# Token rows drifting a tile behind the counts, layers in blocks of two tiles, and table splitting spread over two tiles, in a recommendation kernel

## The chip, the cores and the metric

The kernel runs on one core of one Trainium2 chip. The metric is device time in microseconds (us) of one execution, as the median of several runs, lower being better. Two other numbers go with it: the span of one profiled execution (first to last instruction), and the mean granted clock of the matrix engine, where 1.0 is full speed. Engine names are those of the profile: PE (matrix), PEld (its weight loads), DVE (vector), ACT (scalar), POOL (GpSimd, which issues the gathers here), SP (issues plain DMAs). L318 means line 318 of that kernel; the changed kernel has other line numbers than the kernel before.

## The reference, cut to what matters

For each of 16,384 rows the model averages 32 word vectors of 300 columns from a table of 50,000 rows, averages 20 rows each of three tables of 64 columns, takes one row each of four small tables, and feeds 748 columns through three layers to one sigmoid. A "wide" sum of one-column tables is added to the last logit.

```python
tok = word_emb[token_idx].mean(axis=1)          # 32 of 50000 x 300
e1, e2, e3 = (emb_mh_i[mh_i_idx].mean(axis=1))  # 20 each of 1000, 5000, 10000 x 64
o1 ... o4 = emb_oh_i[oh_i_idx]                  # 100, 50, 20, 1000 x 64
emb = concatenate([tok, e1, e2, e3, o1, o2, o3, o4], axis=1)
wide = sum over all small tables of their wide column, at the same indices
h = relu(emb @ W1 + b1)   # 748 -> 1024
h = relu(h @ W2 + b2)     # -> 512
h = relu(h @ W3 + b3)     # -> 256
return sigmoid(h @ Wd + bd + wide)
```

## The kernel before

A tile is 128 batch rows, and there are 128 of them. The small tables stay in SBUF, split into three bf16 terms. Lookups in them are done as counting (one-hot matrices from DVE, products on PE into `pc`, evicted by ACT as `cnt`) followed by sums of table slices weighted with the counts (PE into `pg`). Word vectors are too many for that: they are gathered by 32 indirect DMAs per tile and added on DVE. Everything is put out in 11 steps per tile, so that each engine has something of each kind to do all the time. In step-tile t, counts belong to tile t, sums to tile t-1 and layers to a block of tiles finished before.

The token part starts a tile's gathers with its counts and adds each group of two rows three groups later:

```python
tokp = tile_pool(name="tok", bufs=2 * TOK_LAG)        # 6 buffers of two rows
def tokens(t, it):
    for q in range(n_groups):                          # 16 groups of 2 gathers
        rows = tokp.tile([P, TOK_GROUP * TOK_D], F32)
        for r in range(TOK_GROUP):
            nc.gpsimd.indirect_dma_start(out=rows[:, r * TOK_D : ...], in_=word, ...)
        under_way.append((t, q, rows))
        if len(under_way) > TOK_LAG:
            add_up(*under_way.pop(0))                  # two DVE additions
        yield 1
# ... in each step i of tile t:
toks.to(n_groups * (i + 1) / STEPS)
```

The layers take blocks of four tiles (512 columns) and, at the end, of two, one and one:

```python
def transposed(x, gs):
    for k in range(NK):                                # 6 chunks of features
        pt = ps_h.tile([P, BLOCK], F32, tag="ph")      # PSUM, 2 buffers
        for s, g in enumerate(gs):
            nc.tensor.transpose(pt[:kk, s * P : (s + 1) * P], chunk(g, k), ident)
        nc.vector.tensor_scalar(x[:kk, k, 0:n], pt[:kk, 0:n], scale[:kk, k : k + 1], None, ALU.mult)
        yield CHUNK_WORK
def layer(dst, weights, bias, src, kks, n_out, n):
    for m in range(n_out):
        ph = ps_h.tile([P, BLOCK], F32, tag="ph")
        for k, kk in enumerate(kks):
            nc.tensor.matmul(ph[:, 0:n], weights[...], src[:kk, k, 0:n], ...)
        nc.scalar.activation(dst[:, m, 0:n], ph[:, 0:n], AF.Relu, bias=...)
sizes = [NSUB] * (tiles // NSUB - 1) + [NSUB - 2, 1, 1]
```

The splitting of the small tables (18 ACT and 12 DVE operations) is done inside tile 0, and counts are evicted with `AF.Copy, scale=0.5, saturate=True`.

## Time and profile before

| | kernel before |
|---|---|
| time, median of 3 runs | 5295.36 us (5286.8 to 5298.4) |
| span of the profiled run, clock | 5284.0 us, 0.991 |
| busy: PE, POOL, DVE, ACT | 96%, 73%, 71%, 48% |
| step-tile 3 begins | 152.5 us |
| step-tile 3 to 125, per tile | 40.06 us |
| from step-tile 125 to the end | 243.9 us |

The last three rows are read from PE's timeline: a new step-tile begins where the 128 count matmuls of the one before are done.

PE is the busiest engine, so one would call it the bound. The chain of work that ended last, followed back from the last instruction, says otherwise (first lines of that view, shares of the span):

```profile
PE 26%; DMA 26%; issue 17%; DVE 17%; POOL 12%; ACT 1%; SPq 0%; DVEq 0%; POOLq 0%; ACTq 0%
```

Only a quarter of the chain is PE. Most of the rest is the loop of gather, landing and addition. The group of DVE's token additions (columns: engine and operation, shapes, count, then busy time and mean duration, then idle time before them and what ended most of it) shows DVE waiting for landings:

```profile
L214 DVE TENSOR_TENSOR own<-own,tok_rows 128x300 f32<-128x300 f32 x1792 | 857.1, 478 | 715.5 <-DMA tok_rows<-in_word_emb_dram,it 684.8
```

Of its idle time 684.8 us end with a landing. Keep this line in mind: it is the one that changes most.

### The profile page before, as it was taken

Reading aid. Unit: us, or ns where it says so; the run is one execution under the profiler, and the core shown is the slowest. Engines: PE = TensorE matmul, PEld = TensorE weight load, DVE = VectorE, ACT = ScalarE, POOL = GpSimd, SP = SyncE. Lnnn points to the kernel's source line nnn. Section 1 sums busy time; section 2 is a strip of 40 time slices with the busy share of each in tenths; the row PEclk is TensorE's granted clock in tenths of the full one; section 3 lists DMA queues with packets and bytes.
Section 4 is the critical chain, followed back from the end, with each engine's and each line's share of the span. In section 5 each row is a group of like instructions: output and inputs, shape, how many; then the busy total and the mean of one; then the engine's idle time right before and its main releaser. Section 6 shows DMA issues by size and latency. Waiting matters only on the chain.

```text
span 5284.0 us, 104301 instructions
## 1 busy us (share of the span) xinstructions
PE 5073.1 (96%) x41320; PEld 3160.4 (60%) x41320; DVE 3763.4 (71%) x8014; ACT 2528.4 (48%) x2000; POOL 3881.2 (73%) x4103
## 2 busy tenths in 40 slices
PE   3699999999999999999999999999999999999999
PEld 3556565666565666666566556556656556655658
DVE  6777777777777777777777777777777777777753
ACT  5444444444444444444444445445444444444433
POOL 5777777777777777777777777777777777777762
PEclk9799999999999999999999999999999999999999
DMA  6444444444444444444444444444444444444431
GB/s 167 125 124 126 126 126 126 126 125 125 126 126 126 126 124 126 126 125 126 125 125 125 126 126 125 124 125 126 125 126 125 124 126 125 126 126 125 124 103 34
DMA packets 245354, 652.60 MB, mean 124 GB/s; under 512 B 108977, under 2 KB 111988, under 8 KB 244863
## 3 DMA queue, kind: packets, MB, share of 16 engines
q0 software_dynamic: 196608, 629.41, 43.4%
q1 hardware_dynamic: 48255, 16.53, 1.4%
q8 instruction: 323, 5.29, 0.4%
q14 instruction: 168, 1.38, 0.1%
HBM read 645.59 MB, written 0.07 MB: 122 GB/s over the span
## 4 chain that ended last, share of the span: by engine, by line
PE 26%; DMA 26%; issue 17%; DVE 17%; POOL 12%; ACT 1%; SPq 0%; DVEq 0%; POOLq 0%; ACTq 0%
DMA tok_rows<-in_word_emb_dram,it 25%; PE ph L387 14%; POOL tok_rows L223 12%; PE pg L336 8%; DVE own L214 5%; DVE own L212 3%; PE pc L311 3%; DVE slice L293 3%; DVE row L293 1%; DVE x L378 1%; DVE g L342 1%; DVE own L210 1%; PE po L412 1%; DMA raw<-in_mh_dram 0%; ACT cnt L318 0%
## 5 line engine op out<-in xcount | busy, mean ns | idle before, releaser
L223 POOL DMA_INDIRECT tok_rows<-in_word_emb_dram,it x4096 | 3880.3, 947 | 1324.0 <-issue 754.2
L318 ACT ACTIVATE cnt<-pc 128x1656 fp8e3<-128x1656 f32 (+1 forms) x1408 | 2120.6, 1506 | 2020.2 <-PE pc L311 2004.1
L336 PE MATMUL pg<-terms,cnt 128*128 128x195 bf16 x17664 | 1847.6, 254 | 83.1 <-DVE g L342 81.4
L336 PEld LDWEIGHTS <-cnt 128*128 128x128 fp8e3 x17664 | 1599.5, 144 | 229.1 <-issue 74.9
L387 PE MATMUL ph<-x,w_sb 128*128 128x512 f32 (+5 forms) x3264 | 1458.3, 576 | 0.5 <-DVE x L378 0.5
L214 DVE TENSOR_TENSOR own<-own,tok_rows 128x300 f32<-128x300 f32 x1792 | 857.1, 478 | 715.5 <-DMA tok_rows<-in_word_emb_dram,it 684.8
L387 PE MATMUL ph<-h,w_sb 128*128 128x512 f32 (+2 forms) x2720 | 1211.0, 573 | 0.0
L212 DVE TENSOR_TENSOR own<-own,tok_rows 128x300 f32<-128x300 f32 x1920 | 918.5, 478 | 400.3 <-DMA tok_rows<-in_word_emb_dram,it 348.6
L311 PEld LDWEIGHTS <-row 64*128 64x128 bf16 x16384 | 504.5, 95 | 1083.3 <-DVE own L214 255.7
L293 DVE TENSOR_TENSOR row<-own,sc 128x768 bf16<-128x768 bf16 (+1 forms) x1408 | 761.3, 541 | 156.5 <-PE pc L311 81.7
L311 PE MATMUL pc<-slice,row 64*128 64x138 bf16 x16384 | 759.1, 224 | 115.0 <-ACT cnt L318 72.2
L387 PEld LDWEIGHTS ph<-x,w_sb 128*128 128x128 f32 (+1 forms) x3264 | 560.3, 193 | 397.8 <-issue 394.0
L293 DVE TENSOR_TENSOR slice<-own,sc 128x828 bf16<-128x828 bf16 (+1 forms) x1408 | 796.2, 565 | 0.0
L387 PEld LDWEIGHTS ph<-h,w_sb 128*128 128x128 f32 x2720 | 463.1, 192 | 318.4 <-issue 316.3
L396 ACT ACTIVATE h<-ph,b_sb 128x512 f32<-128x512 f32 (+2 forms) x476 | 315.3, 662 | 684.8 <-PE ph L387 673.1
L342 DVE TENSOR_REDUCE g<-pg 128x130 f32<-128x390 f32 (+1 forms) x512 | 258.1, 504 | 108.7 <-PE pg L336 108.3
L378 DVE TENSOR_SCALAR x<-pt,scale 128x512 f32<-128x512 f32 (+4 forms) x204 | 137.2, 713 | 5.3 <-PE pt L377 3.4
L377 PE MATMUL pt<-ident,g 128*128 128x128 f32 (+1 forms) x768 | 103.2, 275 | 2.8 <-DVE x L378 2.3
L210 DVE TENSOR_TENSOR own<-tok_rows 128x300 f32<-128x300 f32 x128 | 61.5, 480 | 47.5 <-DMA tok_rows<-in_word_emb_dram,it 44.6
L377 PEld LDWEIGHTS pt<-ident,g 128*128 128x128 f32 (+1 forms) x768 | 85.5, 140 | 6.4 <-DVE x L378 5.4
L214 DVE TENSOR_TENSOR g<-own,tok_rows 128x300 f32<-128x300 f32 x128 | 60.2, 470 | 25.9 <-DMA tok_rows<-in_word_emb_dram,it 21.1
L412 PE MATMUL po<-h,wd_sb 128*1 128x512 f32 (+2 forms) x136 | 60.9, 566 | 0.3
(34 smaller groups left out, 369.1 us busy)
## 6 DMA issues: line engine op xcount, KB each, us to landing
tok_rows<-in_word_emb_dram,it POOLq DMA_INDIRECT x4096
ix<-in_idx_dram SPq DMA_DIRECT2D x128, 32.0 KB
w_sb<-in_W_dram SPq DMA_DIRECT2D x6, 512.0 KB
it<-in_idx_dram SPq DMA_DIRECT2D x32, 64.0 KB
w_sb<-in_W_dram SPq DMA_DIRECT2D x1, 2048.0 KB
raw<-in_mh_dram SPq DMA_DIRECT2D x1, 975.0 KB
out_dram<-h SPq DMA_DIRECT2D x31, 2.0 KB
raw<-in_mh_dram SPq DMA_DIRECT2D x1, 292.5 KB
```

Of the source, the lines that this page charges most:

```text
L212: nc.vector.tensor_add(tok_sum, tok_sum, a)
L214: nc.vector.tensor_add(to, tok_sum, b)
L223: nc.gpsimd.indirect_dma_start(out=rows[:, r * TOK_D : (r + 1) * TOK_D], out_offset=None, in_=word, in_offset=bass.IndirectOffsetOnAxis(ap ...
L293: nc.vector.tensor_tensor(one[:, 0:rows, :].rearrange("p i (n d) -> p i n d", d=2), iota[:, 0:n].rearrange("p (n d) -> p n d", d=2).unsque ...
L311: nc.tensor.matmul(pc[:, f, k // n, at : at + n_h], hot[0][half, k, :], hot[1][half, k, :], start=True, stop=True,)
L318: nc.scalar.activation(cnt[:, :, b : b + rows, :].rearrange("l f (g k) h -> l f g (k h)", g=2), pc[:, :, :, 0 : n * n_h], AF.Copy, scale=0 ...
L336: nc.tensor.matmul(pg[:, j, :], by_slice[:, :, h], terms[:, h, :], start=(h == h0), stop=(h == h1 - 1))
L342: nc.vector.tensor_reduce(g[:, at : at + n * ROW].rearrange("p (f d) -> p f d", f=n), pg[:, 0:n, :].rearrange("p f (c d) -> p f d c", c=3) ...
L377: nc.tensor.transpose(pt[:kk, s * P : (s + 1) * P], chunk(g, k), ident)
L378: nc.vector.tensor_scalar(x[:kk, k, 0:n], pt[:kk, 0:n], scale[:kk, k : k + 1], None, ALU.mult)
L387: nc.tensor.matmul(ph[:, 0:n], weights[:kk, k, m * P : (m + 1) * P], src[:kk, k, 0:n], start=(k == 0), stop=(k == len(kks) - 1),)
L396: nc.scalar.activation(dst[:, m, 0:n], ph[:, 0:n], AF.Relu, bias=bias[:, m : m + 1])
```

## The change

Four things change together. (1) Token groups become one stream over the whole run, spread over 129 step-tiles instead of 128, so that tokens drift slowly until they are a tile behind the counts; eight row buffers instead of six. (2) Layers come in blocks of two tiles (256 columns) throughout, so that less is left over at the end and layers begin earlier. (3) The table splitting is spread over two tiles, with 1.2 of ACT's copies (and the subtraction ahead of each, where there is one) per step from the fourth step on; the weights are loaded a tile later. (4) The saturation flag of the count eviction goes.

```diff
+TOK_BUFS = 8
+LAYER_BLOCK = 256
-CHUNK_WORK = 1
-LAYER_TIME = 10
+CHUNK_WORK = 0.5
+TABLE_PACE = 1.2
+LAYER_TIME = 5
...
-    PART, CHUNK = n_h // 3, n_h // 6
+    PART = n_h // 6
...   (splitting: one ACT copy per yield, DVE's subtraction ahead of it)
+                if c:
+                    nc.vector.scalar_tensor_tensor(rows, rows, 2.0 if c == 1 else 1.0, term[c - 1], ...)
+                nc.scalar.activation(term[c], rows, AF.Copy, scale=2.0 if c == 0 else 1.0)
+                yield 1
...
+    n_all = B // P * n_groups + TOK_LAG
-    def tokens(t, it):
+    def tokens():
+        for n in range(n_all):
+            if n < n_all - TOK_LAG:
+                ... two gathers of group n ...
+            if n >= TOK_LAG:
+                add_up(*under_way.pop(0))
...
-            saturate=True,
+            saturate=False,
...
-            pt = ps_h.tile([P, BLOCK], F32, name="pt", tag="ph")
+            pt = ps_h.tile([P, LAYER_BLOCK], F32, name="pt", tag="ph")
...   (the same for ph, x, h1, h2, h3, po)
-    sizes = [NSUB] * (tiles // NSUB - 1) + [NSUB - 2, 1, 1]
...
-                toks.to(n_groups * (i + 1) / STEPS)
+            toks.to(n_all * (t * STEPS + i + 1) / ((tiles + 1) * STEPS))
-                if t == 0 and i % 3:
-                    next(tables_on_chip, None)
-                if t == 0 and i == STEPS - 1:
+                tables_on_chip.to(TABLE_PACE * (t * STEPS + i - 2))
+                if t == 1 and i == STEPS - 1:
                     load_weights()
```

## The prediction

> **What bounds the kernel now.** One core walks 128 tiles of 128 batch rows in 11 steps each. A step counts lookups (PE into `pc`, ACT evicts), sums table slices (PE into `pg`), runs some matmuls of the layers, and adds gathered token rows on DVE; 32 gathers per tile are issued on POOL. I read the page's groups first, then the windows, then POOL's and PE's timelines in mid run and near both ends.
>
> ```profile
> L223 POOL DMA_INDIRECT tok_rows<-in_word_emb_dram,it x4096 | 3880.3, 947 | 1324.0 <-issue 754.2
> L336 PE MATMUL pg<-terms,cnt 128*128 128x195 bf16 x17664 | 1847.6, 254 | 83.1 <-DVE g L342 81.4
> L387 PE MATMUL ph<-x,w_sb 128*128 128x512 f32 (+5 forms) x3264 | 1458.3, 576 | 0.5 <-DVE x L378 0.5
> ```
> ```profile
> 0.00:50.00 50.00, 6.95 (x88) 5.13 (x88) 26.74 (x59) 24.57 (x17) 23.16 (x29) 1.00 0.76 183
> 1000.00:2000.00 1000.00, 985.86 (x8006) 603.62 (x8003) 729.25 (x1553) 489.07 (x384) 756.35 (x800) 1.00 0.46 125
> ```
> ```profile
> 2021.84 0.94 POOL L223 DMA_INDIRECT tok_rows<-in_word_emb_dram,it  x1 [0.30 <-DVE own L214]
> 2023.09 0.95 POOL L223 DMA_INDIRECT tok_rows<-in_word_emb_dram,it  x1 [0.30 <-issue]
> 2024.34 0.95 POOL L223 DMA_INDIRECT tok_rows<-in_word_emb_dram,it  x1 [0.30 <-DVE own L214]
> ```
>
> PE is busy 98.6% of that window, POOL only 75.6%, and yet POOL is the bound. Gathers start every 1.25 us (0.95 busy, 0.30 between), 800 per 1000 us, with no longer gap from about 76 to 5084 us. 32 x 1.25 = 40.0 us per tile, 4096 x 1.25 = 5120 us in all. PE is a hair behind it, as the timeline's start-to-start distances show (records overlap, so their means do not):
>
> ```profile
> 2020.95 0.54 PE L311 MATMUL pc<-slice,row 64*128 64x138 bf16 x12
> 2021.43 1.52 PE L336 MATMUL pg<-terms,cnt 128*128 128x195 bf16 x15
> 2022.78 1.91 PE L387 MATMUL ph<-x,w_sb 108*128 108x512 f32 x4
> 2024.62 0.54 PE L311 MATMUL pc<-slice,row 64*128 64x138 bf16 x12
> ```
>
> 12 counts take 0.475 us, 15 sums 1.36 (0.085 each and 0.09 handover), four layer records of 512 columns 1.84 (0.432 each and 0.11). Over four tiles of PE: counts 20.4, 552 sums with handovers 50.7, 176 layer records 80.9, transposes 2.9, output row 2.7, keys and the wait for ACT's table loads 1.0: 158.6 us, or 39.65 per tile. Tile starts in the timeline lie 160.3 us apart per four. So in the middle gathers set the pace with some 0.4 us per tile to spare on PE. At the edges POOL is stopped: gather issue loses about 37 us by 76 us (15.3, 3.6 three times, 7.1 and slow gathers), and after 5084 us PE is the bound, since the last layer blocks are of 2, 1 and 1 tiles.
>
> **What the Trainium skill says.** "Perfetto Trace Analysis", DMA Instruction — SWDGE (GPSIMD): a gather's record ends when its last descriptor is written, not when data lands. The trace agrees: the chain of waits has pieces of 3 to 5 us on token rows behind records of 0.95 us. "TensorE: Matmul & The Clock Gate", Back-to-back issue gap: N/2.4 + 2.5 ns, thus 216 ns at 512 columns and 109 at 256. My 432 and, below, 218 ns per f32 record are twice these; halving columns saves nothing per column here. "SBUF — State Buffer", in the text on the shared GPSIMD/Vector port: a DVE operation with two SBUF inputs and a GpSimd operation that reads SBUF exclude each other. The table splitting on DVE does that to gathers:
>
> ```profile
> 39.42 1.72 DVE L175 SCALAR_TENSOR_TENSOR raw<-raw,terms 128x1495 f32<-128x1495 f32 x1 [1.78 <-ACT terms L173]
> 39.49 2.46 POOL L223 DMA_INDIRECT tok_rows<-in_word_emb_dram,it  x1 [0.30 <-issue]
> ```
>
> The gather ends 0.81 us after the DVE operation does. "ScalarE: Activation LUTs", What ACT_TABLE_LOAD costs: 1283 ns; the groups have 64 loads at 1283.
>
> **The change part by part.**
>
> *Token rows.* 2051 turns (2048 groups of two gathers and a lag of 3) are spread over 129 x 11 steps, not 2048 over 128 x 11: 1.445 groups per step against 1.455. Gathers then need 39.75 us per tile of PE order. The number and the 1.25 us stay. A last gather can come late in step-tile 128, so gather-bound the kernel would end about 3 + 5120 + start stalls + 2 landing + 46 (last block, below).
>
> *Layers in blocks of two tiles.* The same columns in twice the records of 256. The old kernel ran one such block near its end, with PE as the bound, so its costs can be read:
>
> ```profile
> 5160.25 0.54 PE L311 MATMUL pc<-slice,row 64*128 64x138 bf16 x12
> 5160.73 1.61 PE L336 MATMUL pg<-terms,cnt 128*128 128x195 bf16 x16
> 5162.18 0.60 PE L377 MATMUL pt<-ident,g 128*128 128x128 f32 x4
> 5163.39 0.83 PE L377 MATMUL pt<-ident,g 128*108 128x128 f32 x4 [0.61 <-DVE x L378]
> 5164.40 0.84 PE L377 MATMUL pt<-ident,g 128*128 128x128 f32 x4 [0.18 <-DVE x L378]
> 5165.41 1.56 PE L387 MATMUL ph<-x,w_sb 128*128 128x256 f32 x6 [0.18 <-DVE x L378]
> ...
> 5178.16 0.54 PE L311 MATMUL pc<-slice,row 64*128 64x138 bf16 x12
> 5178.64 1.52 PE L336 MATMUL pg<-terms,cnt 128*128 128x195 bf16 x15
> 5179.99 3.65 PE L387 MATMUL ph<-x,w_sb 108*128 108x256 f32 x16
> 5183.57 0.54 PE L311 MATMUL pc<-slice,row 64*128 64x138 bf16 x12
> ```
>
> 16 records of 256 take 3.58 us: 0.218 each and 0.09 handover. The twelve transposes take 3.23 us (5162.18 to 5165.41) where PE alone needs about 1.4: with two PSUM buffers they go to and fro with DVE's evictions. The instruction order of the changed kernel shows all twelve in one step of every block; before they were spread two chunks to a step and did not stall. Its 22 steps hold 88 layer matmuls (176 records). The output row took 1.59 us for two tiles.
> PE per two tiles: counts 2 x 5.1 = 10.2; 276 sums 23.4 and 22 handovers 2.0; layers 176 x 0.218 = 38.3 and 2.0; transposes 3.2; output row 1.6; keys 0.1. Sum 80.8, and adding step by step in the new order gives 80.7. That is **40.35 us per tile**, against 39.65 before and the gathers' 39.75. The sum has PE pass gathers as the bound.
> ACT makes relus of 256 (0.47) twice as often as of 512 (0.69), and twice the sigmoid's table loads; at 48% busy this hides, the loads behind the transposes.
>
> *Table splitting over two tiles.* The same 18 ACT and 12 DVE operations, 1.2 per step. A DVE step then has 1.03 (one-hots) + 1.3 + 1.5 (adds) = 3.8 us, near the gathers' 3.6, and eight row buffers in place of six ride over it. The 37 us lost at the start become mostly port conflicts, 12 of about 1 us, and about 5 of stalls. The first layers wait for two tiles, not four. Step-tile 3 begins when group 42 or so of tokens is in: 3 + 44 x 2.5 + 2 = 115, plus 15: about 130 us.
>
> *Plain copies.* The saturation flag goes; the eviction stays one ACT operation of 1.55 us off the path. 0.
>
> **Sum.** Step-tiles 0 to 2: 130. Tiles 3 to 126 are 62 pairs at 80.7: 5003. Tile 127 opens a block: 41.2. Step-tile 128 has no counts: 39.5 - 5.2 = 34.3. The last block alone: transposes 3.2, layers 38.3, output 1.6, sigmoid 0.8, last reductions 0.8, DMA out 2.2 = 46.9. Total 5255 us of span. Timed runs lay 3 to 14 us above the profile's span of 5284.0; I give the time as **5258 us**, 0.7% below 5295.36.
>
> **The rivals.**
> 1. *Gathers stay the bound*, if the DVE and PE dance at block starts shrinks or hides: 3 + 5120 + 15 + 2 + 46 = 5186 of span, some 5190 timed, right at the 2% line (5189.5). For it: no gather was late in 4000. Against it: it needs PE 0.6 us per tile cheaper than steps read from the old trace, where they repeat to 0.02 us.
> 2. *PE is worse than counted*: six evictions queue on DVE behind token adds, or counts wait behind two table loads on ACT at each of 64 block ends. One microsecond more per block is 62 us: about 5320, slower by 0.5%. Against it: the old two-tile block had all these and is in my 3.2 us.
> 3. *The start does not improve*, each DVE splitting stopping POOL and ACT's operations in turn holding counts: up to 25 us more, 5283.
> None passes 2% slower (5401).
>
> **Range and chances.** An error of 0.3 us per tile in PE's sum is 38 us, of the start about 15. I take 5205 to 5300 for 8 in 10. Faster by over 2% asks for rival 1 in full: 0.08. Slower by over 2%: 0.02. Within: 0.90.
>
> **What would show it.** Mid run, fewer than 800 gathers per 1000 us (about 793), POOL waits on DVE adds longer than 0.3 us, and adds that hardly wait for DMA. PE tile pairs 80 to 81.5 us apart, transposes taking about 3.2 us each block. First layer matmul at 125 to 140 us, a last block of about 45 us after the last sum. Wrong if gathers still run at 1.25 us without a break, or pairs lie at 79.5 us; then it is rival 1.

## The result

| | before | after |
|---|---|---|
| time, median of 4 runs | 5295.3 us (5286.8 to 5298.4) | 5280.24 us (5278.8 to 5281.1) |
| span of the profiled run, clock | 5284.0 us, 0.991 | 5278.4 us, 0.996 |
| step-tile 3 begins | 152.5 us | 127.8 us |
| step-tiles 3 to 125 (122 tiles) | 4887.6 us, 40.06 per tile | 4949.9 us, 40.57 per tile |
| from step-tile 125 to the end | 243.9 us | 200.8 us |

The ratio of the times is 0.9974, with a 95% interval of 0.9957 to 0.9991: a small gain, inside the range of the prediction, but little more than a third of the 0.7% that it named. (Ratios here are the mean time of one kernel's fast runs over that of the other's in the same rounds, so they need not equal the ratio of the medians.) The rows of the table add up in the spans: 24.7 us won at the start and 43.2 at the end, 62.3 lost in the middle, in all 5.6. (The medians differ by 15 us. The profiled execution of the kernel before took 5285.8 us and was one of its fastest, so the spans show less.)

Here are the same views of the changed kernel. First the gathers' group, the DVE additions that answer to the line of before, and the chain that ended last:

```profile
PE 95%; DVE 3%; issue 1%; DMA 1%; ACT 0%; POOL 0%; SPq 0%; DVEq 0%; ACTq 0%; POOLq 0%
L230 POOL DMA_INDIRECT tok_rows<-in_word_emb_dram,it x4096 | 3886.9, 949 | 1332.7 <-issue 859.7
L218 DVE TENSOR_TENSOR own<-own,tok_rows 128x300 f32<-128x300 f32 x1792 | 857.1, 478 | 66.7 <-DMA tok_rows<-in_word_emb_dram,it 5.1
```

The idle time of this DVE line that landings ended fell from 684.8 to 5.1 us, and the chain is 95% PE. The gathers themselves cost what they did (949 ns each, 947 before), but they now wait for others. The window of the same thousand microseconds as before (columns: window, its length, busy time and instructions of PE, PEld, DVE, ACT, POOL, then PE's clock, DMA share, GB/s) has 785 gathers instead of 800:

```profile
1000.00:2000.00 1000.00, 987.74 (x9012) 797.43 (x9007) 732.18 (x1566) 495.25 (x458) 741.92 (x785) 1.00 0.45 123
```

So the bound moved from the gathers to PE, as predicted. PE's busy time in the window barely tells it (985.86 before, 987.74 after), since an engine that is just behind the bound looks just as busy.

Now PE's timeline at the start of a layer block (columns: start, duration, engine, line, operation and tiles, count, and in brackets an idle time and what ended it). It repeats in every pair of tiles:

```profile
1997.76 0.54 PE L315 MATMUL pc<-slice,row 64*128 64x138 bf16 x12
1998.23 1.61 PE L340 MATMUL pg<-terms,cnt 128*128 128x195 bf16 x16
1999.68 0.60 PE L380 MATMUL pt<-ident,g 128*128 128x128 f32 x4
2000.89 0.83 PE L380 MATMUL pt<-ident,g 128*108 128x128 f32 x4 [0.61 <-DVE x L381]
2001.90 0.84 PE L380 MATMUL pt<-ident,g 128*128 128x128 f32 x4 [0.18 <-DVE x L381]
2002.91 0.70 PE L390 MATMUL ph<-x,w_sb 128*128 128x256 f32 x2 [0.18 <-DVE x L381]
```

The transposes take 3.23 us (1999.68 to 2002.91), the figure read in advance from the old kernel's one block of two. The step is 5.8 us long where its neighbours take 3.68. Pairs of tiles lie 80.95 us apart, and 81.14 where the four key transposes fall in: 81.05 on the mean of two, where 80.7 was predicted.

The first pair (step-tiles 3 and 4) took 86.7 us. In its first steps PE ran at half its clock (granted 0.50 from 121 to 140 us):

```profile
127.77 0.87 PE L315 MATMUL pc<-slice,row 64*128 64x138 bf16 x12 [0.64 <-DVE slice L297]
...
134.73 1.10 PE L380 MATMUL pt<-ident,g 128*108 128x128 f32 x4 [1.96 <-DVE x L381]
...
143.03 0.54 PE L315 MATMUL pc<-slice,row 64*128 64x138 bf16 x12
```

Twelve counts take 0.87 us until 138 us and 0.54 from 143 us on. Before the pair, without layers to do, PE was busy for only 15.4 us of the 28 from 100 to 128 us. PE's waits in this pair come to 3.4 us, where a later pair has 1.0; so of the 5.7 us that it is longer, some 2.4 are waits, and the rest is work at the lower clock.

One line that nobody had asked for: ACT's table loads in the changed kernel.

```profile
L322 ACT ACT_TABLE_LOAD x1 | 1.3, 1283 | 0.7 <-PEq L547 0.7
L422 ACT ACT_TABLE_LOAD x1 | 1.3, 1283 | 0.0
```

The kernel before had 32 of 1283 ns at the eviction and 32 at the sigmoid. The prediction had expected twice as many.

### The profile page after: what moved, and what is told of

The parts are those of the page before. It is cut to its first block, busy times and chain, and to the rows that moved or that the text cites. A ratio compares the mean times of both kernels' runs of the same rounds, so it can differ in the third digit from the quotient of the medians.

```text
span 5278.4 us, 115771 instructions
## 1 busy us (share of the span) xinstructions
PE 5140.1 (97%) x46720; PEld 4154.7 (79%) x46720; DVE 3838.0 (73%) x8194; ACT 2590.6 (49%) x2388; POOL 3887.8 (74%) x4103
## 4 chain that ended last, share of the span: by engine, by line
PE 95%; DVE 3%; issue 1%; DMA 1%; ACT 0%; POOL 0%; SPq 0%; DVEq 0%; ACTq 0%; POOLq 0%
PE ph L390 47%; PE pg L340 32%; PE pc L315 12%; DVE x L381 2%; PE po L414 1%; PE pt L380 1%; PE po L418 1%; DVE g L346 0%; DMA tok_rows<-in_word_emb_dram,it 0%; DVE own L218 0%; DVE own L216 0%; PE pk L280 0%; DVE slice L297 0%; DMA raw<-in_mh_dram 0%; ACT cnt L322 0%
## 5 line engine op out<-in xcount | busy, mean ns | idle before, releaser
L390 PE MATMUL ph<-x,w_sb 128*128 128x256 f32 (+1 forms) x6144 | 1476.2, 383 | 11.0 <-DVE x L381 10.8
L390 PEld LDWEIGHTS ph<-x,w_sb 128*128 128x128 f32 (+1 forms) x6144 | 1111.4, 191 | 148.1 <-DVE x L381 26.3
L390 PE MATMUL ph<-h,w_sb 128*128 128x256 f32 x5120 | 1224.5, 382 | 0.0
L390 PEld LDWEIGHTS ph<-h,w_sb 128*128 128x128 f32 x5120 | 927.9, 191 | 99.6
L399 ACT ACTIVATE h<-ph,b_sb 128x256 f32<-128x256 f32 x896 | 423.8, 473 | 798.9 <-PE ph L390 798.9
L380 PE MATMUL pt<-ident,g 128*128 128x128 f32 (+1 forms) x768 | 146.6, 293 | 51.6 <-DVE x L381 51.1
L381 DVE TENSOR_SCALAR x<-pt,scale 128x256 f32<-128x256 f32 (+1 forms) x384 | 169.2, 481 | 20.4 <-PE pt L380 3.9
L414 PE MATMUL po<-h,wd_sb 128*1 128x256 f32 x256 | 75.8, 377 | 2.6
L422 ACT ACTIVATE h<-po,bd_sb 1x256 f32<-1x256 f32 x64 | 29.7, 464 | 70.5 <-PE po L418 70.5
```

The source lines that it names most:

```text
L381: nc.vector.tensor_scalar(x[:kk, k, :], pt[:kk, :], scale[:kk, k : k + 1], None, ALU.mult)
L390: nc.tensor.matmul(ph, weights[:kk, k, m * P : (m + 1) * P], src[:kk, k, :], start=(k == 0), stop=(k == len(kks) - 1),)
L399: nc.scalar.activation(dst[:, m, :], ph, AF.Relu, bias=bias[:, m : m + 1])
```

## The experiments

The theory A to be tested: in the changed kernel PE sets the pace with 81.05 us per pair; of that, the blocks of two cost the most, partly through the back and forth of transposes and copies at each block's start; the start and the end gain from the staggered splitting and the smaller last block. Rivals: B, the gathers or their landings are still part of the pace; C, the drift or the splitting cost PE time; D, the waits at block starts are hidden anyway or only move.

### All gathers: another state on four chips

The first job took four variants of the changed kernel with all their gathers:

```diff
e1_spread, e1_again:  -CHUNK_WORK = 0.5
                      +CHUNK_WORK = 2                     # transposes over several steps
e2_nodrift:           -toks.to(n_all * (t * STEPS + i + 1) / ((tiles + 1) * STEPS))
                      +toks.to(n_groups * (t + (i + 1) / STEPS) if t < tiles else n_all)
e3_tables:            the kernel before's table splitting, all in tile 0
e4_saturate:          -saturate=False
                      +saturate=True
```

> The changed kernel with CHUNK_WORK 2 in place of 0.5, so that the pace puts about two transpose chunks into a step, as the kernel before had it, and not all six into one. Theory A (PE is the bound, and the bunched transposes cost it about 1.8 us per pair of tiles): transposes cost about 0.97 us per two chunks, a pair of tiles falls from 81.05 to about 79.3 us, and gathers become the bound again, at 39.7 us per tile. Time about 5280 - 62 x 1.5 = 5187, 5178 to 5205. Rival B (the pair is long because 256-column records cost more by themselves, and the stall fills with other work): pairs stay at 80.8 or more, time 5270 to 5285.

> The changed kernel with its token rows paced as before, 16 groups within each tile's own 11 steps, no drift. Theory A (PE, not the gathers, bounds the middle at 40.5 us per tile, so the drift has nothing to give here): gathers need 40.0 us per tile, still under 40.5; time 5272 to 5292. Rival B (the drift is where the gain over the kernel before comes from): mid run at the gathers' pace with waits, time over 5305.

> The changed kernel with the table splitting of the kernel before, all within the first tile, in parts of 46 slices. Theory A (a PE-bound run keeps whatever the start loses): step-tile 3 begins some 20 to 30 us later than 127.8 us and the end moves by the same; time 5298 to 5312. Rival B (the start hides behind gathers that run ahead): under 5288.

> The changed kernel with the saturation flag back on the count evictions. The profile of the changed kernel has 2 activation table loads, that of before 64, so I expect about 128 loads of 1.28 us to come back, two at each of 64 block ends. Theory A (ScalarE has the room, the loads lie behind the transposes that PE does with VectorE): time within 6 us of 5280. Rival B (counts wait for ScalarE at each block end, as the 0.74 us at a block end of the kernel before): 64 x 0.74 = 47 us more, 5327.

> The first four runs fell on a chip whose granted clock was 0.88 to 0.90 and on which the kernel before itself took 7181 us, so none of their expectations, all for a chip at 0.99, was tested. This is the first of them again: CHUNK_WORK 2, transposes spread two chunks to a step. On a chip where the kernel before takes some 5295: theory A (bunched transposes cost about 1.8 us per pair, gathers become the bound again at 39.7 us per tile): 5178 to 5205, ratio to before about 0.980. Rival B (256-column records are what costs): pairs stay at 80.8 or more, 5270 to 5285, ratio 0.997.

None of these expectations could be tested. On that chip the kernel before itself took 7181 us at a clock of 0.90, not 5295, and the same held on all four chips of the later jobs (7153 to 7199 us). The variants took 7373 us (e1, ratio 1.027; 7374 and 1.025 when repeated), 7443 (e2, 1.036), 7520 (e3, 1.047) and 7500 (e4, 1.045). The changed kernel as it is was run as a control later:

> The changed kernel, unedited, as the control of this chip. If the kernel before comes to some 5295 us here, this chip is like the first one and the changed kernel should come to 5280 (ratio 0.997). If the kernel before comes to some 7180 at a clock near 0.90, as on the chip of the earlier experiments, the theory that full gather traffic holds this chip up for both kernels expects the changed kernel between 7370 and 7550, as its four relatives were, with the halved runs of this job near 5200 to 5310 all the same; the rival, that the earlier four edits themselves cost the time, expects a ratio of 0.997 again.

It took 7399 us against 7153, ratio 1.034 (1.030 to 1.038). So in this state the change loses 3.4%, and the variants' times come from the state first of all. Its window and its chain:

```profile
1000.00:2000.00 1000.00, 815.67 (x6461) 635.90 (x6459) 524.53 (x1123) 351.19 (x329) 532.62 (x561) 0.89 0.33 88
PE 55%; another core or an unknown queue 17%; DVE 15%; issue 11%; ACT 2%; DVEq 0%; SPq 0%; DMA 0%; ACTq 0%
```

There are 561 gathers per 1000 us instead of 785, data come at 88 GB/s instead of 123, and 17% of the chain are waits whose releaser the trace doesn't hold. It isn't word rows that are late: gathers take 951 ns each as before, and of the idle time ahead of the two large groups of token additions less than 1 us each ends with a landing. The cause of this state stays open. Since times of this state say nothing of the first measurement, the questions were put in another way.

### Half the gathers: a state that can be compared

If each group gathers one row and adds it twice, instruction streams of PE, DVE and ACT stay the same while POOL and the DMA engines do half the work. The token part of the result is then wrong on purpose (the comparison with the reference passed all the same, so it is not sensitive to that part).

```diff
-        a, b = rows[:, 0:TOK_D], rows[:, TOK_D : 2 * TOK_D]
+        a, b = rows[:, 0:TOK_D], rows[:, 0:TOK_D]
-                for r in range(TOK_GROUP):
+                for r in range(TOK_GROUP)[::TOK_GROUP]:
```

> The changed kernel with half its gathers (one row per group, added twice; wrong result on purpose), all else alike, vector work included. On a chip where the kernel before takes some 5295. Theory A (the changed kernel's middle is bound by PE): pairs of tiles stay at 80.9 to 81.2 us, the start shortens a little, time 5255 to 5282. Rival B (gathers still bind the middle): pairs fall well under 80 and the time under 5200. If the chip is again the one at a clock of 0.89, the run only shows that.

It took 5285.92 us at a clock of 0.997, on a chip where the kernel before with all gathers took 7181. That is 4 us above theory A's range. The shortest pairs of tiles lie 80.95 and 81.14 us apart, as in the changed kernel's trace; others are up to 0.5 us longer, and the mean from step-tile 5 on is 81.24 us against 81.05. With POOL busy 37% of the time instead of 74% nothing got faster: PE's own work is the changed kernel's pace, and rival B falls for it. Half gathers also lift the slow state, so all that follows is compared at half gathers.

The same for the kernel before:

> The kernel before with half its gathers, each row added twice (results wrong on purpose in the token part). The theory of the prediction is that gathers at 1.25 us were the bound (160.3 us per four tiles) and PE needs 158.6: with half the gathers four tiles should lie 158.4 to 158.9 us apart, and the run take 52 us off the middle and up to 35 off the start: 5200 to 5235 us. The rival, that PE or its waits set the old pace already, expects 160.3 us per four tiles and 5275 to 5295.

It took 5182.94 us, and four tiles lie 157.85 us apart: theory A's direction, and both numbers a little below its ranges. This window of it is PE at its limit, 995 of 1000 us:

```profile
1000.00:2000.00 1000.00, 995.04 (x8109) 610.07 (x8108) 751.22 (x1586) 492.95 (x386) 385.00 (x408) 1.00 0.24 65
```

So before the change PE alone needed 157.85 us per four tiles and the gathers held it at 160.3; after it PE needs 2 x 81.05 = 162.1. The change put PE's floor above the pace at which gathers had held the kernel. This is where the gain of the start and the end went: 122 tiles at 0.51 us more.

### Which part carries PE's loss

The kernel before, with drift, staggered splitting and plain copies, but blocks of four as before (and with its six row buffers), at half gathers:

> The kernel before with the change's token drift, staggered table splitting and plain copies, but the layers left in blocks of four tiles, with half the gathers. The theory that the blocks of two alone raise PE's time (157.85 us per four tiles measured with blocks of four, 162.1 with two) expects 157.7 to 158.0 per four tiles again and, with an earlier start, 5155 to 5180 us against 5183 for the kernel before at half its gathers. The rival, that drift or splitting costs PE time too, expects over 158.5 per four tiles and over 5190.

It took 5172.71 us, with 157.9 us per four tiles at the median. Drift and splitting cost PE nothing, and rival C falls: the blocks of two carry the 4.2 us per four tiles (the eight row buffers, the one other difference to the changed kernel that bears on tokens, had no run of their own). PE's start-to-start distances say where: per pair of tiles, from e6 to the changed kernel, transposes go from 1.85 to 3.24 us, layers from 40.29 to 40.77, the output row from 1.34 to 1.60, while counts and sums stay within 0.02. Two thirds of the loss are the transposes.

Against e6 the run is 10 us shorter: step-tile 3 begins 15.8 us earlier, but from step-tile 125 to the end it takes 252.1 us, 8.1 more than e6. In e5, with blocks of two, that end takes 200.8 us. So the gain at the end comes with the blocks of two. What the drift gives with all gathers stays open, since e2 and e14 ran in the slow state only.

The changed kernel with the old splitting, at half gathers:

> The changed kernel with half its gathers, but the table splitting of the kernel before (all of it inside the first tile). If the staggered splitting is what shortens the start, step-tile 3 begins 20 to 35 us later than its 124.7 us, and the run takes 5305 to 5320. If the earlier first layer block alone shortens it (two tiles awaited, not four), it is within 8 us: 5278 to 5294. Pairs stay at 80.95 and 81.14 us in both.

It took 5301.1 us, 15.2 more than e5. Step-tile 3 began at 140.8 us instead of 124.4 (in e8 on the same chip). The expectation of 20 to 35 us was too high, but the staggered splitting it is that shortens the start, by 15 to 16 us. In e6, the kernel before at half gathers, step-tile 3 began at 140.0 us, so at half gathers this is all of the gain at the start. With all gathers it is 24.7 us, and there the traces show gathers setting the pace: up to 130 us their issue lost 35.7 us before the change (32.0 in stalls, 3.7 in slow gathers) and 11.4 after it (0.4 and 11.0). Which of the changes ended the stalls, the splitting, the drift or the two more row buffers, no run with all gathers in the state of the first measurement tells.

The saturation flag again, at half gathers:

> The changed kernel with half its gathers and the saturation flag on the count evictions again. The theory expects ACT's table loads to come back at both ends of each of 64 output rows (about 128 loads of 1.28 us, some 160 us of ACT that is 49% busy) without a cost: 5280 to 5292 us, pairs within 0.1. The rival, that counts wait behind two loads once a block, expects 0.4 to 0.8 us per block: 5310 to 5335.

It took 5286.96 us, 1.0 more than e5, with pairs of 80.95 and 81.15. The loads are all back:

```profile
L322 ACT ACT_TABLE_LOAD x63 | 80.8, 1283 | 1.8 <-PEq L547 0.7
L422 ACT ACT_TABLE_LOAD x63 | 80.8, 1283 | 1.1
```

So it is the flag that brings them, 126 of them cost 161.6 us of ACT, and they are hidden. The Trainium skill, "ScalarE: Activation LUTs", Table sets: the hidden batching unit, says that cheap functions, copy among them, are in every set. The two loads of the plain eviction agree with it; the copy with saturation behaves like a function of another set.

### What the back and forth at a block's start costs

Transposes over several steps, at half gathers (`CHUNK_WORK = 2`):

> The changed kernel with half its gathers (5286 us, pairs of tiles 80.95 and 81.14 us apart) and in addition the pace of the transposes set so that a step holds at most two chunks of them. The theory that PE is the bound and that the twelve bunched transposes wait some 1.8 us a block for DVE's copies out of PSUM expects pairs of 79.2 to 79.6 us and 62 times 1.6 less: 5170 to 5200 us. The rival, that the waits only move (the third chunk waits for DVE in another step, as 2 us did in one block start of an earlier run), expects pairs of 80.5 to 81.2 and 5255 to 5290.

It took 5284.83 us, 1.1 us less than e5: the rival's expectation. Its timeline shows one reason:

```profile
2077.06 0.54 PE L315 MATMUL pc<-slice,row 64*128 64x138 bf16 x12
2077.70 1.46 PE L340 MATMUL pg<-terms,cnt 128*128 128x195 bf16 x15
2079.01 0.60 PE L380 MATMUL pt<-ident,g 128*108 128x128 f32 x4
2080.86 0.44 PE L380 MATMUL pt<-ident,g 128*128 128x128 f32 x2 [1.26 <-DVE x L381]
```

Steps without layer matmuls are short for PE, about 2.5 us, while DVE's one-hots, additions and copies take longer, so PE waits for the copy here (1.26 us in one step) instead of there. The waits only moved, as rival D has it: those over 0.1 us come to 1.53 us per pair on the mean, against 1.14 in e5.

The other reason is the clock. In the changed kernel and in e5 it stays at full speed from 141 us to the last microseconds. In e8 it falls to half 17 times between step-tiles 5 and 125, for 3.41 us each time, as here, where 15 sums take 2.53 us instead of 1.52:

```profile
1024.72 0.44 PE L380 MATMUL pt<-ident,g 128*128 128x128 f32 x2 [2.03 <-DVE x L381]
1025.57 2.53 PE L340 MATMUL pg<-terms,cnt 128*128 128x195 bf16 x15
```

The 17 pairs with such a stretch take 82.80 us on the mean, the other 43 take 80.59, where e5's mean is 81.24. Waits left out, the means are 80.79 and 79.25, so the lower clock cost about 1.5 us each time, an estimated 26 us in all. Without it the edit would have gained that much, still far from theory A's 100 us. All four timed executions have a clock of 0.991 to 0.993, against 0.997 in e5. Why the clock falls no run tested.

Two chunks per PSUM buffer, each with its own copy, so that four chunks fit in the two buffers:

```diff
-            pt = ps_h.tile([P, LAYER_BLOCK], F32, name="pt", tag="ph")
+            if k % 2 == 0:
+                two = ps_h.tile([P, 2 * LAYER_BLOCK], F32, name="pt", tag="ph")
+            pt = two[:, k % 2 * LAYER_BLOCK : (k % 2 + 1) * LAYER_BLOCK]
```

> The changed kernel with half its gathers (5286 us), with two transposed chunks per PSUM buffer, so that four chunks can be under way before PE waits for DVE's copies. The theory that the back and forth between PE and DVE at a block's start lengthens PE's pair by some 1.2 to 1.6 us expects the step with the twelve transposes at 4.2 to 4.6 us in place of 5.79, pairs of 79.5 to 79.9 us and 62 times 1.2 to 1.6 less: 5187 to 5215 us. The rival, that DVE's own work per step (six copies of 0.48 us on top of one-hots and adds) holds PE up anyway in the next steps, expects pairs within 0.4 us of 81.05 and 5262 to 5290.

It took 5374.18 us, 88 us more, against both expectations. The timeline:

```profile
2026.32 0.38 PE L382 MATMUL pt<-ident,g 128*128 128x128 f32 x2
2027.53 0.66 PE L382 MATMUL pt<-ident,g 128*128 128x128 f32 x4 [0.83 <-DVE x L383]
2028.94 0.66 PE L382 MATMUL pt<-ident,g 128*128 128x128 f32 x4 [0.75 <-DVE x L383]
2030.35 0.44 PE L382 MATMUL pt<-ident,g 128*128 128x128 f32 x2 [0.75 <-DVE x L383]
```

PE now waits three times for 0.75 to 0.83 us: the second chunk of a buffer doesn't begin before DVE has copied the first, though it goes to other columns. The Trainium skill, "PSUM — Partial Sum Buffer", PSUM bank collisions raise a hardware error, says that two engines must not touch one bank in the same quarter of the partitions at a time, whether or not they touch the same bytes, and that PSUM is to be guarded by bank and quarter, or more simply by bank. The trace agrees with such a guard: the transposes of the second chunk wait for the copy of the first. No run here left the guard out. The failed edit is useful in another way. It lengthened the waits in each block by 0.97 us (pairs at 81.93 and 82.12), and the run grew by 62 x 0.97 = 60 us and 28 more. These 28 are nearly all the clock's: 13 pairs hold a stretch at half clock and take 84.2 us on the mean, the others 82.2, which makes 26 us. A wait added at a block's start goes into the time in full.

With all gathers the same edit told nothing more; the slow state was there, and 7602 us against 7199 lie even above what was expected of it:

> The changed kernel with all its gathers and two transposed chunks per PSUM buffer. If this chip runs the kernel before at about 5295 us, the theory expects PE to fall just under the gathers, which then are the bound at 40.0 us a tile: pairs of 80.0 to 80.2 and 5190 to 5220 us (ratio 0.980 to 0.986), faster than both kernels; the rival expects 5265 to 5290. If the kernel before takes about 7150 us here, as in the last jobs, gathers hold everything up and this run can't tell: 7350 to 7450 us.

The wait taken away in earnest: one copy for two chunks, after the transposes of both. The scale that differed by chunk is folded once into the first weights (six DVE operations in step-tile 2).

```diff
+        for ks in ((0, 1), (3, 4), (5, 2)):
+            two = ps_h.tile([P, 2, LAYER_BLOCK], F32, name="pt", tag="ph")
+            ... the four transposes of both chunks ...
+            nc.vector.tensor_copy(x[:, ks[0] : ks[0] + 2, :], two)   # (5, 2): two copies
+            yield 2 * CHUNK_WORK
+                if t == 2 and i >= STEPS - NK:      # once, before the first layers
+                    nc.vector.tensor_scalar(w, w, scale[: chunk_k[k], k : k + 1], None, ALU.mult)
```

> The changed kernel with half its gathers, with the input scale folded once into the first weights, so that a plain copy of 512 columns takes two transposed chunks out of PSUM at a time, and all four transposes of a buffer come before its copies. The last attempt put two chunks into one buffer with a copy each; PE then waited after every chunk and the pair grew by 0.97 us. If it is the back and forth that costs, one wait of about 0.6 us is left where there were 1.65 us: the step with the transposes takes 4.5 to 5.0 us in place of 5.79, pairs lie 79.9 to 80.4 apart on the mean, and the run takes 5210 to 5250 us against 5286. The rival, that DVE's whole work and not the alternation holds PE up, expects 5270 to 5290.

It took 5212.2 us, 73.7 less than e5, with pairs of 79.77 and 79.96 us. The transposes go through both buffers, wait once, and are done:

```profile
2053.54 1.04 PE L381 MATMUL pt<-ident,g 128*128 128x128 f32 x8
2055.38 0.66 PE L381 MATMUL pt<-ident,g 128*128 128x128 f32 x4 [0.80 <-DVE x L386]
2055.97 0.70 PE L393 MATMUL ph<-x,w_sb 128*128 128x256 f32 x2
```

All twelve transposes take 2.43 us here instead of 3.23; on the mean over the run they take 2.21 where e5 has 3.41, and the other parts of a pair agree within 0.01. Pairs fell by 1.18 us (on the mean from 81.24 to 80.05), and 62 x 1.18 = 73 is the gain measured. So the back and forth is real time on PE, some 1.2 us of each pair. The edit also leaves DVE four copies a block instead of six, 2.2 us in place of 2.9; how much comes from the order and how much from the fewer copies was not tested apart.

The same with all gathers, and blocks of four with all gathers, for the version that might beat both kernels:

> The same with all its gathers. On a chip where the kernel before takes about 5295 us: PE and the gathers are level at 40.0 us a tile, 5205 to 5245 us. Where the kernel before takes about 7180, gathers hold everything up: 7350 to 7600 us, no verdict on the transposes.

> All gathers, the layers in blocks of four tiles as before, with the drift, the staggered splitting and the plain copies of the change. Where the kernel before takes about 5295 us: the gathers keep the middle at 160.3 us per four tiles and only the start gains, 5260 to 5280 us, level with or just below the changed kernel. Where it takes about 7180: if it is the layers in blocks of two that make the changed kernel worse there (it came to 7400, ratio 1.034), this one lies near the kernel before, ratio 0.985 to 1.005; if the drift or the splitting does, ratio 1.02 to 1.05.

e17 took 7437 us against 7190 (ratio 1.034), e14 took 7236 (1.007, 1.005 to 1.009). The slow state was there again. e17 came out as expected for it, e14 just above its range of 0.985 to 1.005. Blocks of two lose 2.5% (e1) to 5.7% (e12) there whatever is done about their transposes; blocks of four lie near the kernel before. So no version with all gathers was shown to beat both kernels. For the state of the first measurement an estimate is all there is: PE at e16's mean of 80.05 us per pair would be level with the gathers' 80.0 (64 of them at 1.25), so the pairs could shrink from 81.05 to a little over 80, some 60 us at most over 61 pairs.

## Why the prediction was right or wrong, point by point

- **Gathers bound the kernel before, PE a hair behind: right, the distance mis-sized.** PE's floor was predicted at 158.6 us per four tiles; half the gathers measured 157.85 (transposes took 3.7 us, not 2.9; sums, layers and the last item less than counted). The slack was 0.6 us per tile, not 0.4.
- **PE becomes the bound: right.** The chain is 95% PE, additions no longer wait for landings, and half the gathers don't make the pairs shorter. Rival 1 of the prediction (gathers stay the bound) did not happen; what came is a mild form of rival 2 (PE worse than counted), with a third of the microsecond per block that it named.
- **The sum per pair of tiles: wrong in size, and this is the step that failed.** The prediction put it as "PE per two tiles: counts 2 x 5.1 = 10.2; 276 sums 23.4 and 22 handovers 2.0; layers 176 x 0.218 = 38.3 and 2.0; transposes 3.2 ... and adding step by step in the new order gives 80.7". Start-to-start distances in the changed kernel give counts 10.21, sums 25.13 (not 25.4), layers 40.77 (not 40.3), transposes 3.24, output row 1.60, keys 0.12: 81.05 with rounding. The term that is off is the layers' handover to the next step. Eight records of 256 take 1.849 us and twelve 2.715, thus 0.216 each and 0.12 for the handover, where 0.09 was taken over from one old step. There are 22 steps per pair, and the layers come out 0.47 us above the sum; the sums give back 0.27, small items add 0.05, and the lower of two totals (80.7, not 80.8) was chosen. In all 0.35 us per pair are missing, or 21.5 us over 61 pairs.
- **"Tiles 3 to 126 are 62 pairs at 80.7": wrong for the first.** It took 86.7 us, 5.7 more than a later pair. By the trace some 2.4 of these are waits, the longest of 1.96 us for a copy, and the rest is work at half clock after a start with little load. Together with the point above this makes 27.2 us, all that the middle was longer than predicted.
- **Start and end: right.** Step-tile 3 was predicted at about 130 us and began at 127.8; of the 12 port conflicts of about 1 us and 5 us of stalls in it, the trace has 12 slow gathers (11.0 us in all) and hardly any stall (0.4 us). From step-tile 125 on the terms of the prediction add up to 80.7 + 41.2 + 34.3 + 46.9 = 203.1 us, and 200.8 were measured. Of the start, the staggered splitting is worth 15 us at half gathers (e9); the end gains by the blocks of two (e15 against e5).
- **Plain copies: right, at half gathers, that they cost and gain nothing, wrong in what they do.** The prediction expected twice the table loads; the flag's removal took away all but two. e10 shows that the loads were hidden. In the slow state the changed kernel's ratio was 1.045 with the flag (e4) and 1.034 without (e11), on two chips; this was not followed up.
- **Why so little error matters so much.** The forecast gain of 29 us in span was itself a difference: against the old trace its terms win 22.5 us at the start (152.5 - 130) and 40.8 at the end (243.9 - 203.1), and lose 35.1 in the middle (61 x 80.7 - 4887.6). An error of 0.4% in the one term that repeats 62 times took most of it.

## What to carry to other kernels

When a change is meant to lift a bound, measure the next engine's floor before counting the gain: halving the work of the bound, even with a wrong result, shows that floor in one run, and here it showed that smaller blocks had raised it above the old bound. A term that repeats some sixty times wants its handovers fitted from several groups of different size, not from one, when the gain forecast is below a percent. A run that comes out level can be a gain and a loss: read the granted clock of its trace before calling an edit useless. And PSUM buffers that hand over between two engines did best here filled whole and emptied in one operation; two halves of one bank were no double buffer.

## What the Trainium skill lacked or had wrong

- "ScalarE: Activation LUTs", Table sets: it says that copy is in every set and doesn't speak of the saturation flag. With the flag a copy next to a sigmoid brought 63 loads at each of the two lines, 1283 ns each; without it 1 and 1.
- "PSUM — Partial Sum Buffer", PSUM bank collisions raise a hardware error: it doesn't tell what keeping engines apart costs in time. Here each change of turn between PE and DVE on one bank left PE idle for 0.75 to 0.83 us.
- "TensorE: Matmul & The Clock Gate", Back-to-back issue gap: the section gives no time for f32, nor for the change from one kind of matmul to the next. Records of 256 f32 columns (two to a matmul) came every 0.216 us, and a group of them cost 0.12 us on top before the next bf16 counts.
- We found no page that explains the slow state: with all gathers the kernel before took 7153 to 7199 us on four chips and 5295 in the first measurement; with half of them it took 5183 us at a clock of 0.997.
